# A second Strassen level for three of seven block products, with norm statistics on ScalarE

## The chip, the cores and the metric

The kernel runs on one core of a Trainium2 chip, in float32. The metric is the device time of one execution in microseconds (us). TensorE (PE in the profile) multiplies matrices into the banks of PSUM, VectorE (DVE) and ScalarE (ACT) read and write both PSUM and the on-chip memory SBUF, [...] and SyncE (SP) issues the transfers. Each engine runs its own queue of instructions in order and waits for the others by semaphores.

## The reference, cut to what matters

Sixteen batches of 1024 nodes with 512 features pass two layers that share one 1024x1024 adjacency matrix.

```python
h = relu(layernorm(x))                       # layer 0
x = x + einsum('nm,bmd->bnd', adj, h) @ W0 + bias
h = relu(layernorm(x))                       # layer 1
g = h @ W
e = leaky_relu(g @ a1 [:, None] + g @ a2 [None, :], 0.2) * adj
x = x + elu(softmax(e) @ g + beta * g)
```

The change touches layer 0 and the norm that opens layer 1. There u stands for `relu(layernorm(x))` of layer 0's output.

## The kernel before, in words

Both products of a layer, the one with the adjacency (or the attention matrix) and the one with the weight, are computed by a Strassen scheme of the Winograd form: the left and right factor are cut into 2x2 blocks, seven block products (`PRODUCTS`, p1 to p7) take the place of eight, and sums of blocks (S1, S2, S3, S4 of the left factor, T1 to T4 of the right) are made on VectorE. For layer 0 the first product is `products_a`: h is the left factor (its blocks A11, A12, A22, S1 to S4 are 128x4 chunks of 256 features), the transposed adjacency is the right one (`adjT`), and it stays in SBUF for all sixteen batches. A block product there is two output halves p of four matmuls k, each of 512 columns. The products accumulate in PSUM banks named by kind, Y, W and X, one for each p: p1, p6, p7 and p4 add to Y, p2 to W, p5 and p3 to X. After each half, a reading instruction takes the partial sum out: a ScalarE copy for p1 (into C11), p6 (C12), p5 (C22) and p4 (C21), a VectorE addition for p2, p7 and p3. The second product is `products_b`: its steps, numbered 0 to 13 (product n, half q: 2n+q), are four matmuls of 256 columns each, and VectorE adds every result to the residual tile xr. xr holds x with the bias added.

The order is written by hand. `tc.keep_in_program_order` keeps each engine's instructions as the program has them, and a plan, a table from step numbers to functions, says what other work is issued after which step of a product (-1 is before the first). Batch b's layer 0 is `layer0_a` with the plans of the last batch's output (`plan_out`) and of the next batch's norm (`plan_norm_a`), then `layer0_b` with the rest of that norm (`plan_norm_b`). All of it passes through one helper, line 109, so the profile has line 109 for every instruction and groups are told apart by tile names: y is the first product of layer 0, po its second; z and pq are layer 1's.

The output of layer 0 is handled by `LayerOut`: `keep` stores xr to DRAM as x1, `stats` takes the norm's mean and variance with VectorE's bn_stats and bn_aggr (lines 220 to 223), `inv_std` (212) makes the scale r and the shift nb from them on GpSimd, `relu` writes u to a tile of its own on ScalarE, `logits` multiplies each u chunk with two vectors on VectorE with an accumulator, `sums` makes the left blocks of u, and `store` sends u and its sums to DRAM for layer 1, which runs after all of layer 0. In `plan_out` all four halves of this stand at the start of the next batch.

Of the kernel before, what the change touches and what calls it, by code (L numbers as in the profile page):

```python
# [59 lines left out]
def kernel(  # L60
# [55 lines left out]
        dve.tensor_tensor(o, i0, i1, op=op)  # L116


    def products_a(name, a_blk, b_blk, after):


        c = new_c(name)
        s = {}
        banks = {}
        for n, (prod, an, bn, kind, first, last) in enumerate(PRODUCTS):
            for p in range(2):
                if first:
                    banks[kind, p] = bank(f"{name}_{kind}{p}")
                ps = banks[kind, p]
                for k in range(HC):  # L130
                    pe.matmul(
                        ps, a_blk(an, k)[:, ts(p, P)], b_blk(bn, k),
                        start=(first and k == 0), stop=(last and k == HC - 1),
                        skip_group_check=True,
                    )
                c11, c12, c21, c22 = (c[k][:, p, :] for k in ("C11", "C12", "C21", "C22"))
                if prod == "p1":
                    act.copy(c11, ps)
                elif prod == "p2":
                    add(c11, ps, c11)  # L140
                elif prod == "p6":
                    act.copy(c12, ps)
                elif prod == "p5":
                    act.copy(c22, ps)
                elif prod == "p7":
                    add(c22, ps, c22)
                elif prod == "p3":
                    if not s:
                        for k in ("S1", "S2", "S4"):
                            s[k] = b4.tile([P, 2, 512], F32, tag="b4", name=f"{name}_{k}")  # L150
                    s1, s2 = s["S1"][:, p, :], s["S2"][:, p, :]
                    add(c12, ps, c12)
                    add(s1, c12, c22)
                    add(s2, s1, c11, ALU.subtract)
                    add(c12, c11, c12, ALU.subtract)
                else:
                    act.copy(c21, ps)
                    add(s["S4"][:, p, :], c21, s["S2"][:, p, :], ALU.subtract)
                after(2 * n + p)
        return {  # L160
            "A11": c["C11"], "A12": c["C21"], "S3": c["C12"], "A22": c["C22"],
            "S1": s["S1"], "S2": s["S2"], "S4": s["S4"],
        }

    def new_c(name):
        return {
# [42 lines left out]
        add(t4, b21, t2, ALU.subtract)  # L209


    def inv_std(r, nb, mv):

        k = r.shape[1]
        pool.tensor_scalar(r, mv[:, :, 1], EPS, 1.0, op0=ALU.add, op1=ALU.mult)
        pool.tensor_tensor(r, r, half[:, 0:k], op=ALU.pow)
        pool.tensor_scalar(nb, mv[:, :, 0], -1.0, 1.0, op0=ALU.mult, op1=ALU.mult)
        pool.tensor_tensor(nb, nb, r, op=ALU.mult)
# [6 lines left out]
    class Norm:  # L225


        def __init__(self, name, src, dst):
            self.name, self.src, self.dst = name, src, dst
            self.n = src.shape[1]  # L230

        def stats(self):
            mv = stat.tile([P, self.n, 2], F32, tag="mv", name=f"mv_{self.name}")
            for k in range(self.n):
                stats(mv[:, k, :], self.src[:, k, :])
            self.r = stat.tile([P, self.n], F32, tag="r", name=f"r_{self.name}", bufs=3)
            self.nb = stat.tile([P, self.n], F32, tag="nb", name=f"nb_{self.name}", bufs=3)
            inv_std(self.r, self.nb, mv)

        def relu(self, c=slice(None)):  # L240
            for k in range(self.n):
                act.activation(
                    self.dst[:, k, c], self.src[:, k, c], AF.Relu,
                    scale=self.r[:, k : k + 1], bias=self.nb[:, k : k + 1],
                )

    def node_rows(t, b):

# [12 lines left out]
    def h_stats(b, k):  # L261
# [2 lines left out]
            hs[b, k // 2] = b8.tile([P, HC, D], F32, tag="b8", name=f"h_{b}_{k // 2}")  # L264
        dst = hs[b, k // 2][:, ts(k % 2, 2), :]
        h_norms[b, k] = Norm(f"h{b}_{k}", xs.pop((b, k)), dst)
        h_norms[b, k].stats()

    def h_relu(b, k):
        h_norms.pop((b, k)).relu()  # L270
# [72 lines left out]
    class LayerOut:  # L343
# [16 lines left out]
            sp.dma_start(out=x1d[self.b][nh, q], in_=xr.rearrange("p k d -> p (k d)"))  # L360

        def stats(self, nh, q):
            xr = xrs.pop((self.b, nh, q))
            if not self.us:
                self.s = {
                    n: up.tile([P, HC, HD], F32, tag="up", name=f"u{n}_{self.b}")
                    for n in ("S1", "S2", "S4")
                }
            self.us[nh, q] = up.tile([P, 2, D], F32, tag="up", name=f"u_{self.b}_{nh}_{q}")
            self.norms[nh, q] = Norm(f"u{self.b}_{nh}_{q}", xr, self.us[nh, q])  # L370
            self.norms[nh, q].stats()

        def relu(self, nh, q):
            self.norms[nh, q].relu()

        def logits(self, nh, q):
            junk = self.s["S1"].rearrange("p k d -> p (k d)")[:, 0:D]
            for k in range(2):
                self.logit_parts(4 * nh + 2 * q + k, self.us[nh, q][:, k, :], junk, v_bcs)

# [392 lines left out]
    def logit_weights(k):  # L773

        v = stat.tile([P, DC], F32, tag="v", name=f"v_{k}")
        junk = up.tile([P, D], F32, tag="up", name=f"junk_{k}")
        for dc in range(DC):
            dve.tensor_tensor_reduce(
                out=junk, in0=w1_t[:, dc, :], in1=v_bcs[k], scale=1.0, scalar=0.0,
                op0=ALU.mult, op1=ALU.add, accum_out=v[:, dc : dc + 1],  # L780
            )
        vd[k] = dram.tile([D], F32, name=f"vd_{k}")
# [31 lines left out]
    def plan_first():  # L814
        return {
            1: [(h_sums, 0, 0), (transpose_adj, 0, 1), (transpose_adj, 1, 0), (h_sums, 0, 1)]
            + [(transpose_adj, 1, 1), (adj_sum, "T1"), (adj_sum, "T2")],
            4: [(adj_sum, "T3")], 5: [(adj_sum, "T4")], 7: [(w_sums, w0_c)],
            12: [(add_bias, 0, 0, 0)], 13: [(add_bias, 0, 0, 1)],
        }  # L820

    def plan_out(o, b):

        plan = {
            -1: [(o.keep, 0, 0), (o.stats, 0, 0), (o.keep, 0, 1), (o.stats, 0, 1)],
            0: [(o.relu, 0, 0), (o.keep, 1, 0), (o.stats, 1, 0)],
            1: [(o.relu, 0, 1), (o.keep, 1, 1), (o.stats, 1, 1)],
            2: [(o.relu, 1, 0)], 3: [(o.relu, 1, 1)],
        }

        for i, (nh, q) in enumerate(halves):
            plan.setdefault((4 if b == 1 else 2) + i, []).append((o.logits, nh, q))
        for q in range(2):
            plan.setdefault((8 if b == 1 else 6) + q, []).extend([(o.sums, q), (o.store, q)])
        for i, (nh, q) in enumerate(halves):
            plan.setdefault(3 + i, []).append((load_res, b, nh, q))
            plan.setdefault(6 + i, []).append((add_bias, b, nh, q))
        return plan

    def plan_norm_a(b):  # L840
        return {
            8: [(h_stats, b, 0), (h_stats, b, 1)],
            9: [(h_relu, b, 0), (h_relu, b, 1), (load_x, b, 2), (load_x, b, 3)],
            12: [(h_stats, b, 2)], 13: [(h_stats, b, 3), (h_relu, b, 2)],
        }

    def plan_norm_b(b):
        plan = {0: [(h_relu, b, 3)], 2: [(h_sums, b, 0)], 5: [(h_sums, b, 1)]}
        if b + 1 < B:
            plan[7] = [(load_x, b + 1, 0), (load_x, b + 1, 1)]  # L850
        return plan

    def plan_softmax(order, s):
# [30 lines left out]
        11: {4: "e6", 8: "M6 K6 e7", 11: "M7 K7 x"}, 13: {9: "N n"},  # L884
    }
    FIRST_A = {
        -1: "R0 R1 R2 R3", 2: "B E0", 3: "E1 R4", 4: "E2 R5", 5: "E3 R6 S", 6: "b E4 R7",
        7: "E5", 8: "E6", 9: "E7 s", 10: "D", 12: "T1a", 13: "T1b",
    }
    FIRST_B = {0: "d", 1: "T2a", 2: "T2b", 4: "T3a", 5: "T3b"}  # L890
    LOADS_U = {5: ("U00",), 7: ("U01",), 9: ("U10", "U11"), 11: ("S2",), 13: ("S1", "S4")}


    sms = [Softmax(b) for b in range(B)]
    for b in range(B):
        plans = [plan_first() if b == 0 else plan_out(LayerOut(b - 1), b)]
        if b + 1 < B:
            plans.append(plan_norm_a(b + 1))
            if b == 1:
                plans.append({2: [(logit_weights_back, 0), (logit_weights_back, 1)]})  # L900
            plan_b = merged(plan_norm_b(b + 1), plan_softmax(EARLY_B.get(b, {}), sms[0]))
            if b == 0:
                plan_b = merged(
                    {2: [(add_bias, 0, 1, 0), (add_bias, 0, 1, 1)]}, plan_b,
                    {9: [(logit_weights, 0)], 11: [(logit_weights, 1)]},
                )
        else:
            plans.insert(0, plan_softmax(FIRST_A, sms[0]))
            plans.append({
                8: [(load_u, 0, ("U00", "U01"))],  # L910
                10: [(load_u, 0, ("U10", "U11", "S2", "S1", "S4"))],
            })
            plan_b = merged(plan_softmax(FIRST_B, sms[0]), plan_softmax(LOGITS_B, sms[1]))
        if 0 < b <= G:
            plans.append({13: [(store_mask, b - 1)]})
        layer0_a(b, merged(*plans))
        layer0_b(b, plan_b)


# [67 lines left out]
```

## Time and profile before

| | us |
|---|---|
| median of 3 runs | 2359.93 (2355.52 to 2363.56) |
| profiled execution | 2366.53 |
| its span | 2364.8 |
| TensorE busy | 2336.3 |
| VectorE busy | 1860.9 |
| ScalarE busy | 1072.2 |
| layer 0, one batch in the middle | 72.24 |

The span runs from the first to the last instruction of one profiled execution. Layer 0 takes about the first half of it, 16 batches until 1186 us; layer 1 follows. One matmul of the program is two records in the profile. "Idle before" is the time in which an engine had nothing to do before an instruction, and the arrow names what ended it.

### The profile page before, as it was taken

To read this page: it belongs to the slowest core of one execution; us is meant where nothing else is said; L and a number is where in the kernel's file an instruction comes from. 1 tells how busy PE (TensorE), PEld (TensorE's weight loads), DVE (VectorE), ACT (ScalarE), POOL (GpSimd) and SP (SyncE) were. 2 spreads that over 40 slices of the span, in tenths; PEclk is the share of its full clock that TensorE was granted. 3 is DMA by queue.
4 is the path that set the end of the run, shared out by engine and by line. 5 is a ranking of instruction groups with operands and counts; after the bars stand their busy time and mean duration, and the time that the engine had idled before them with its cause. 6 is when DMAs were issued, how large, how long until landed. Compare 5 with 4: busy or idle time off the path is not lost.

```text
span 2364.8 us, 26003 instructions
## 1 busy us (share of the span) xinstructions
PE 2336.3 (99%) x7264; PEld 1374.3 (58%) x7264; DVE 1860.9 (79%) x3950; ACT 1072.2 (45%) x2675; POOL 561.9 (24%) x732
## 2 busy tenths in 40 slices
PE   9989999999999999999999999999999999999998
PEld 5655566655566655666555666556665566655565
DVE  5788777888888888788968787877877788777774
ACT  3212222222222232222456676667766676666743
POOL 1223323223222233232102221122211222102220
PEclk9999999999999999999999999999999999999999
DMA  6444434434345455345554556555565554565541
GB/s 218 105 150 155 154 117 166 154 125 158 135 145 200 153 174 179 102 148 179 199 189 147 168 190 203 183 166 174 186 211 171 190 159 159 176 191 154 177 125 42
DMA packets 207234, 382.99 MB, mean 162 GB/s; under 512 B 80240, under 2 KB 88432, under 8 KB 207088
## 3 DMA queue, kind: packets, MB, share of 16 engines
q1 hardware_dynamic: 206768, 380.81, 49.8%
q8 instruction: 57, 0.93, 0.2%
q14 instruction: 89, 0.73, 0.1%
q10 hardware_dynamic: 320, 0.52, 0.1%
HBM read 251.92 MB, written 133.50 MB: 163 GB/s over the span
## 4 chain that ended last, share of the span: by engine, by line
PE 63%; DMA 11%; DVE 10%; ACT 10%; SPq 3%; issue 2%; POOL 1%; DVEq 0%; ACTq 0%
PE y_Y L109 18%; PE po_Y L109 9%; PE y_X L109 9%; PE z_Y L109 7%; ACT e L109 5%; PE po_X L109 5%; PE y_W L109 4%; DVE e L109 4%; DMA md<-mx 4%; PE z_X L109 3%; SPq L109 3%; PE pq_Y L109 3%; PE po_W L109 2%; DMA sd<-sm 2%; PE z_W L109 2%
## 5 line engine op out<-in xcount | busy, mean ns | idle before, releaser
L109 POOL TENSOR_TENSOR x<-x,r 128x512 f32<-128x512 f32 x120 | 226.3, 1896 | 899.7 <-DMA ul_S<-ud_S 400.9
L109 ACT ACTIVATE e<-e,nm 128x256 f32<-128x256 f32 x480 | 238.0, 504 | 166.8 <-DVE nm L109 166.8
L109 ACT COPY y_C<-y_Y 128x512 f32<-128x512 f32 x96 | 56.3, 586 | 543.5 <-PE y_Y L109 534.9
L109 DVE CUSTOM_DVE_ANT_0 e<-e,mask 128x256 f32<-128x256 f32 x512 | 233.7, 508 | 77.4 <-DMA mask<-maskd 40.0
L109 DVE CUSTOM_DVE_ANT_0 uS<-u,v_bc 128x512 f32<-128x512 f32 x240 | 242.7, 1011 | 22.7 <-DMA v_bc<-vd 6.3
L109 PE MATMUL y_Y<-adjT_B,h 128*128 128x512 f32 x512 | 226.8, 596 | 2.4 <-ACT adjT_B L109 2.4
L109 PE MATMUL z_Y<-pT,ul_U 128*128 128x512 f32 x512 | 224.9, 592 | 0.0
L109 ACT ACTIVATE e<-s2b,s1b 128x256 f32<-128x256 f32 x512 | 215.3, 512 | 16.1 <-DVE xr L109 16.1
L109 DVE STREAM_TRANSPOSE pT<-e 128x512 f32<-128x512 f32 x240 | 155.8, 688 | 69.3 <-ACT e L109 69.2
L109 ACT ACTIVATE h<-x,nb_h,r_h 128x512 f32<-128x512 f32 (+1 forms) x132 | 98.6, 795 | 225.4 <-POOL nb_h L109 215.1
L109 PE MATMUL pq_Y<-w_c,z_C 128*128 128x256 f32 x768 | 176.8, 381 | 1.3
L109 PE MATMUL po_Y<-w_c,y_C 128*128 128x256 f32 x768 | 173.6, 379 | 0.0
L109 POOL TENSOR_TENSOR xr<-xr,bias_bc 128x1024 f32<-128x1024 f32 x60 | 151.9, 2540 | 68.7 <-DMA xr<-in_x_dram 67.4
L109 PEld LDWEIGHTS y_Y<-adjT_B,h 128*128 128x128 f32 x512 | 97.8, 191 | 119.3 <-issue 115.4
L109 PEld LDWEIGHTS z_Y<-pT,ul_U 128*128 128x128 f32 x512 | 97.3, 190 | 115.6 <-issue 112.4
L109 PEld LDWEIGHTS pq_Y<-w_c,z_C 128*128 128x128 f32 x768 | 144.6, 190 | 32.6 <-issue 7.7
L109 PEld LDWEIGHTS po_Y<-w_c,y_C 128*128 128x128 f32 x768 | 145.9, 190 | 26.7 <-issue 7.7
L109 ACT ACTIVATE r<-z,rs 128x256 f32<-128x256 f32 x192 | 96.1, 500 | 109.6 <-DVE z L109 109.6
L109 DVE TENSOR_TENSOR xr<-po_Y,xr 128x512 f32<-128x512 f32 x128 | 86.4, 688 | 55.5 <-PE po_Y L109 55.5
L109 PE MATMUL po_X<-w_c,y_S 128*128 128x256 f32 x512 | 115.7, 379 | 0.0
L109 PE MATMUL pq_X<-w_c,z_S 128*128 128x256 f32 x512 | 115.6, 379 | 0.0
L109 PE MATMUL y_Y<-adjT_T,h 128*128 128x512 f32 x256 | 112.7, 592 | 1.5 <-DVE y_C L109 1.5
(127 smaller groups left out, 4172.8 us busy)
## 6 DMA issues: line engine op xcount, KB each, us to landing
mask<-maskd SPq DMA_DIRECT2D x128, 512.0 KB
x<-in_x_dram SPq DMA_DIRECT2D x64, 512.0 KB
xr<-in_x_dram SPq DMA_DIRECT2D x256, 128.0 KB
x1d<-xr SPq DMA_DIRECT2D x64, 512.0 KB
ul_U<-ud_U SPq DMA_DIRECT2D x64, 512.0 KB
x<-x1d SPq DMA_DIRECT2D x64, 512.0 KB
out_dram<-x SPq DMA_DIRECT2D x252, 128.0 KB
ud_U<-u SPq DMA_DIRECT2D x60, 512.0 KB
```

The costliest lines, as they stand in the source:

```text
L109: return lambda *args, **kwargs: tc.keep_in_program_order(f(*args, **kwargs))
```

## The change

In batches 1 to 15 of layer 0, p1, p5 and p3 are each computed by the same scheme once more: seven inner products, r1 to r7, each of two matmuls with 256 columns. Their left factors are quarters of the left block and three sums of them (`inner_left`, VectorE, for every batch), their right factors quarters of the adjacency block and three more tiles, which are made once (`inner_right`, `exts`). The result lands in the same banks Y and X, with help of one more bank, y, and for p3 a further one, x. r1, r6 and r7 accumulate in y, and between them ScalarE copies y (after r1), VectorE adds y and an inner sum (after r6), and ScalarE copies y again (after r7); then VectorE adds to the bank of half 0 (after r7) and half 1 (after r3). A paired product, p2, p6 or p7, which stays as it was, gives one matmul between any two inner steps: the matmuls of a group stand in the order r1, plain, r4, plain, r5, plain, r6, plain, plain, r7, plain, r2, plain, r3, plain, and p4 follows the three groups.

The norms' statistics (except those of batch 0 and a late part of the last batch) go from VectorE to ScalarE: sums by an Identity with accumulator, then the squares around the mean by Square. The statistics of layer 0's output are issued from step 11 of the second product on, as the halves become ready, and the last at -1. u is written over xr, so the residual's next load into that buffer comes after u's store. The plans are set anew, and the first softmax's diagonal and sums go from the last batch's first product to its second.

```diff
+    def products_a2(name, a_blk, b_blk, inner, after):
+        read = ReadA(name)
...
+            y = bank(f"{name}_{prod}y")[:, 0:256]
+            x = i0[:, 256:512] if first else bank(f"{name}_{prod}x")[:, 0:256]
+            t = b4.tile([P, 4, 256], F32, tag="b4", name=f"{name}_{prod}t")
...
+            outs = {
+                "r1": (y, True), "r4": (i0[:, 0:256], first), "r5": (x, not first),
+                "r6": (y, False), "r7": (y, False), "r2": (i1[:, 0:256], first),
+                "r3": (i1[:, 256:512], False),
+            }
...
+                if r == "r1":
+                    act.copy(t[:, 0, :], y)
+                elif r == "r5":
+                    act.copy(t5, x)
+                elif r == "r6":
+                    add(t[:, 1, :], y, t5)
+                elif r == "r7":
+                    act.copy(t[:, 2, :], y)
+                    if first:
+                        i0v = i0.rearrange("p (a n) -> p a n", a=2)
+                        add(i0v, i0v, t[:, 2:3, :].to_broadcast([P, 2, 256]))
+                    else:
+                        add(t[:, 3, :], y, t5)
+                        add(i0, i0, t[:, 2:4, :].rearrange("p a n -> p (a n)"))
+                elif r == "r3":
+                    add(i1, i1, t[:, 0:2, :].rearrange("p a n -> p (a n)"))
...
+        for two, one in (("p1", "p2"), ("p5", "p6"), ("p3", "p7")):
+            inn, pla = inner_steps(two), plain_steps(one)
+            for m in range(4):
+                inn[m]()
+                if m == 2:
+                    after(k)
+                pla[m]()
+            pla[4]()
+            if one != "p2":
+                reads(one, 0)
+            inn[4]()
+            pla[5]()
+            reads(two, 0)
+            if one == "p2":
+                reads(one, 0)
+            after(k + 1)
+            inn[5]()
+            pla[6]()
+            after(k + 2)
+            inn[6]()
+            pla[7]()
...
+            after(k + 3)
+            k += 4
...
+    def inner_left(b, prod):
+        left = hs[b][{"p1": "A11", "p5": "S1", "p3": "S4"}[prod]]
+        s = b4.tile([P, 4, 2, P], F32, tag="b4", name=f"in_{b}_{prod}")
...
+        add(s[:, 0], a21, a22)
+        add(s[:, 1], s[:, 0], a11, ALU.subtract)
+        add(a21, a11, a21, ALU.subtract)
+        add(s[:, 2], a12, s[:, 1], ALU.subtract)
...
+        def sums(self):
+            mv = stat.tile([P, 3, self.n], F32, tag="mv", name=f"mv_{self.name}")
+            for k in range(self.n):
+                act.activation(
+                    junk, self.src[:, k, :], AF.Identity, accum_out=mv[:, 0, k : k + 1]
+                )
+            act.activation(mv[:, 1, :], mv[:, 0, :], AF.Copy, scale=-1.0 / D)
+            for k in range(self.n):
+                act.activation(
+                    junk, self.src[:, k, :], AF.Square, bias=mv[:, 1, k : k + 1],
+                    accum_out=mv[:, 2, k : k + 1],
+                )
...
-            self.us[nh, q] = up.tile([P, 2, D], F32, tag="up", name=f"u_{self.b}_{nh}_{q}")
-            self.norms[nh, q] = Norm(f"u{self.b}_{nh}_{q}", xr, self.us[nh, q])
-            self.norms[nh, q].stats()
+            self.us[nh, q] = xr
+            self.norms[nh, q] = Norm(f"u{self.b}_{nh}_{q}", xr, xr)
+            self.norms[nh, q].sums()
...
+        late = 2 if b == 1 else 0
+        plan = {}
+        for k, step in (
+            (-1, (o.stats, 1, 1)), (-1, (o.keep, 0, 0)), (-1, (o.keep, 1, 0)),
+            (-1, (o.keep, 0, 1)), (-1, (o.keep, 1, 1)),
+            (0, (o.relu, 0, 0)), (1, (o.relu, 1, 0)), (2, (o.relu, 0, 1)), (3, (o.relu, 1, 1)),
+            (2 + late, (o.logits, 0, 0)), (3 + late, (o.logits, 1, 0)),
+            (4 + late, (o.sums, 0)), (4 + late, (o.store, 0)),
+            (5 + late, (o.logits, 0, 1)), (5 + late, (load_res, b, 0, 0)),
+            (6 + late, (o.logits, 1, 1)), (6 + late, (load_res, b, 1, 0)),
+            (7 + late, (o.sums, 1)), (7 + late, (o.store, 1)),
+            (8 + late, (load_res, b, 0, 1)), (9 + late, (load_res, b, 1, 1)),
+        ):
+            plan.setdefault(k, []).append(step)
+        for k, (nh, q) in ((9, (0, 0)), (11, (0, 1)), (12, (1, 0)), (13, (1, 1))):
+            plan.setdefault(k, []).append((add_bias, b, nh, q))
...
     def plan_norm_a(b):
-            8: [(h_stats, b, 0), (h_stats, b, 1)],
-            9: [(h_relu, b, 0), (h_relu, b, 1), (load_x, b, 2), (load_x, b, 3)],
-            12: [(h_stats, b, 2)], 13: [(h_stats, b, 3), (h_relu, b, 2)],
+            7: [(h_stats, b, 0)], 8: [(h_stats, b, 1)],
+            9: [(h_relu, b, 0)], 10: [(h_relu, b, 1), (load_x, b, 2)], 11: [(load_x, b, 3)],
...
     def plan_norm_b(b):
-        plan = {0: [(h_relu, b, 3)], 2: [(h_sums, b, 0)], 5: [(h_sums, b, 1)]}
+            0: [(h_stats, b, 2)], 1: [(h_stats, b, 3)], 3: [(h_relu, b, 2)], 4: [(h_relu, b, 3)],
+            5: [(h_sums, b, 0)], 7: [(h_sums, b, 1)], 9: [(inner_left, b, "p1")],
...
+            plan_b = merged(plan_b, {
+                11: [(out_of.stats, 0, 0)], 12: [(out_of.stats, 0, 1)],
+                13: [(out_of.stats, 1, 0)],
+            })
...
+            plans.append({1: [(inner_left, b, "p5")], 5: [(inner_left, b, "p3")]})
+        (layer0_a2 if b else layer0_a)(b, merged(*plans))
```

`ReadA` holds the reading instructions of `products_a`, which are unchanged. `inner_right` is `inner_left` on the adjacency blocks B11, T1 and B22 with 512-wide sums.

## The prediction

> **What bounds the kernel now.** I read the page's totals, then the windows of one batch of layer 0, then the order of time on each engine inside it, then the rows that price an instruction.
>
> ```profile
> PE 2336.3 (99%) x7264; PEld 1374.3 (58%) x7264; DVE 1860.9 (79%) x3950; ACT 1072.2 (45%) x2675; POOL 561.9 (24%) x732
> PE 63%; DMA 11%; DVE 10%; ACT 10%; SPq 3%; issue 2%; POOL 1%; DVEq 0%; ACTq 0%
> ```
>
> TensorE is never idle for long: a matmul saved is time saved, and a wait put on TensorE is time lost. The windows (busy time per engine) cut layer 0 at its period of 72.24 us a batch:
>
> ```profile
> 247.24:319.48 72.24, 72.24 (x225) 42.56 (x225) 58.94 (x110) 16.53 (x24) 20.99 (x37) 1.00 0.47 154
> 608.43:680.67 72.24, 72.24 (x225) 42.56 (x225) 61.79 (x126) 19.74 (x32) 21.26 (x37) 1.00 0.44 145
> ```
>
> TensorE 72.24 of 72.24, VectorE 59, ScalarE 16.5. Two pieces of the chain price the matmuls; one program matmul is two records, so sixteen records are one block product (512 columns) or two steps of the second product (256):
>
> ```profile
> 326.34 6.87 PE y_W L109 x16
> 74.23 3.45 PE po_Y L109 x16
> ```
>
> That is 0.859 us for a 128x512 matmul and 0.43 for a 128x256 one. ScalarE at a batch start (order of time), where it has little to do:
>
> ```profile
> 611.90 0.59 ACT L109 COPY y_C<-y_Y 128x512 f32<-128x512 f32 x1 [21.38 <-PE y_Y L109]
> 612.55 1.52 ACT L109 ACTIVATE u<-xr,nb_u,r_u 128x512 f32<-128x512 f32 x2
> 615.33 0.59 ACT L109 COPY y_C<-y_Y 128x512 f32<-128x512 f32 x1 [1.26 <-PE y_Y L109]
> 615.82 4.34 ACT L109 ACTIVATE u<-xr,nb_u,r_u 128x512 f32<-128x512 f32 x6
> ```
>
> Prices: a group row for an activation with two per-partition operands, then accumulating exponentials in order of time on ScalarE, then logits on VectorE:
>
> ```profile
> L109 ACT ACTIVATE h<-x,nb_h,r_h 128x512 f32<-128x512 f32 x124 | 94.3, 808 | 222.9 <-POOL nb_h L109 212.6 <-DMA ud_U<-u 10.2
> ...
> 1508.19 0.51 ACT L109 ACTIVATE e<-e,nm 128x256 f32<-128x256 f32 x1
> 1508.59 0.20 ACT L109 ACTIVATION_READ_ACCUMULATOR e<-e,nm 128x1 f32 x1
> 1508.69 0.51 ACT L109 ACTIVATE e<-e,nm 128x256 f32<-128x256 f32 x1
> ...
> 780.33 0.69 DVE L109 CUSTOM_DVE_ANT_0 uS<-u,v_bc 128x512 f32<-128x512 f32 x1
> 780.95 0.08 DVE L109 DVE_READ_ACCUMULATOR2_ANT s<- 128x1 f32 x1
> 781.17 0.69 DVE L109 CUSTOM_DVE_ANT_0 uS<-u,v_bc 128x512 f32<-128x512 f32 x1
> ```
>
> An accumulator read starts 0.1 before its activation ends and ends 0.1 after. And TensorE once, after the only long gap in layer 0:
>
> ```profile
> 144.61 3.62 PE L109 MATMUL po_W<-w_c,y_C 128*128 128x256 f32 x16
> 155.15 6.03 PE L109 MATMUL po_Y<-w_c,y_S 128*128 128x256 f32 x16 [6.92 <-DVE xr L109]
> 161.01 3.62 PE L109 MATMUL po_X<-w_c,y_S 128*128 128x256 f32 x16
> ```
>
> A gap of 6.92 us costs another 2.4: the next sixteen take 6.03 for 3.62.
>
> [...]
>
> **The change, part by part.** Only batches 1 to 15 change in steady state.
>
> Removed on TensorE: a product of 8 matmuls of 512 columns (6.87) becomes 7 steps r1 to r7 of two 256-column ones (7 x 0.86 = 6.0). Three products a batch: 2.6 us, in 15 batches 39 us.
>
> VectorE: out go 16 statistics pairs (0.67 + 0.18 each, 13.6). In come twelve 256-wide sums of the inner left factors (three times 1.6 with their waits) and four 256- and six 512-wide additions of the steps (5.8). Net about -3: no loss in sum.
>
> ScalarE: out none; in, per norm half (h and u, 8 a batch), two Identity and two Square with accumulator and one 2-element Copy. [...] I take 3.4. In sum 16.5 + 27 + 4 (nine inner copies) is below 70. So sums hide everything; order does not. All queues run in program order, so I lay the new order out from a batch's start (0), in slots of 0.86:
>
> First group (p1 with p2). r6 (slot 6, due at 5.15) accumulates into the bank that r1 wrote, so it waits for ScalarE's copy of r1. In ScalarE's queue four u statistics stand ahead of that copy. The first needs the residual half finished by step 10 of the second product before, 5.17 before the batch start, and VectorE has 1.6 of inner sums ahead of that addition: it starts at -3.7. Four at 3.4 end at 10.0, the copy at 10.4. **Stall 5.2.**
>
> Then VectorE, idle until now, has in order: r6's addition 0.4; wait for r7 and its copy until 14.3; bank addition 0.7; wait for ScalarE's C11 copy 0.6; C11 0.7; inner sums 1.6; four logits at 0.79, 3.2; second bank and C11 with ScalarE's copy between, 2.0; four logits 3.2; left sums 2.5 (638 to 640 in the trace). It reaches p5's r6 addition at 28.9, done 29.3. p5's r7 waits for that. Without a stall TensorE would be there 18 slots (15.5) after r6, at 25.9. **Stall 3.4**, about 1 of it already at p5's r6, as the last u relu (1.5) precedes that copy.
>
> p5's first bank 31.4, logits 3.2, inner sums 1.6, logits 3.2, second bank: 40.1. ScalarE copies it (40.7), then comes h statistics (44.1), then p3's copy of r1 (44.5). r6 of p3, due at 39.7, waits: **stall 4.9**. Behind a waiting r6 stands all of TensorE's queue; behind ScalarE's copy that waits for VectorE stand the u relus that the logits read, and the next copy of r1, which is how one lateness feeds the next. The rest has room: p4's copies, h statistics 2 and 3 (due by step 5, five microseconds later than ready by the same ledger).
>
> Sum 13.5. Cold clock after gaps near 5 us: between 0 and 2.4 for each of two gaps, since the only example had 6.9; I take 1.5 a batch. Net 15.0 - 2.6 = 12.4, times 15: +186.
>
> Once: 12 inner right sums on VectorE at 0.69, 8.3, in batch 0, where VectorE is busy 123 of 175 us; 0 to 8, I take 2. Last batch: exponentials and transposes of the first softmax stand among these steps (four transposes pairs of 1.4 before the third stall, no h statistics): +4; its moved sums and loads of u hide beside 24 us of products, else some 3 to 10. Together +6.
>
> Costed at nothing: fewer small POOL operations (no one waits at the end of POOL's queue); u in the residual's place, whose next load now waits on SP for u's store. By the ledger the store goes at 43 and the first user, step 1 of the second product, comes at 63; some 20 us cover two transfers. Uncovered, a load late by x delays step 1's addition by x.
>
> Sum: 2366.5 (profiled execution) + 192 = 2558; that execution is 6.6 above the median of 2359.9, so 2552 against the median.
>
> **Rivals.**
> - First stall alone: VectorE catches up because it has 20 us idle in a batch. For: its sum is lower than before. Against: the idle time lies before r6, and the logits cannot pass r6's addition in the queue. 5.2 + 2.4 cold - 2.6 = 5.0 a batch, +81: 2441.
> - Cold after both long gaps: 13.5 + 4.8, and the slow r6 to r7 passes 1 more through the chain; net 16.7, +256: 2616.
> - Faster: TensorE's waits at r6 and r7 are met by earlier instructions than I take, so it does not stall. Place: these six points; it decides where all stalls of a batch sum to less than 2.6. For: TensorE had no such idle time before, under the same helpers. Against: r6 writes what the copy must read first. -39 + 2: 2323.
> - Not doing what it says: the built order has the 14 small matmuls for each of three products, so I give it nothing.
>
> **How the numbers follow.** Main case 0.64 (its own range 2480 to 2610: five statistics on the path, so 0.7 less or 0.8 more of each is 3.5 to 4 us a batch and some 55 in all; the cold clock widens it little), first stall alone 0.13, both cold 0.14, faster 0.05, between (within 0.3%, about what a measurement can tell from no change, or just above) 0.04. Faster 0.06, same 0.02, slower 0.92. The range 2425 to 2635 takes in the second and third case.
>
> **What would show it.** Right: a batch period near 85 us; gaps of TensorE of 3 to 6 us on the y banks, put down to ScalarE's copy at r6 of p1 and p3, to VectorE at r7 of p5; [...] clock under 1.00 in layer 0; layer 1 as before. Wrong: a period under 75, four u statistics done by 5 us, or the logits split around the steps.

## The result, and the profile after

The changed kernel takes 2572.8 us (median; 2566.9 to 2573.9), the kernel before 2361.6 beside it: ratio 1.0894, 95% interval 1.0867 to 1.0921. The profiled span went from 2364.8 to 2571.7. The forecast was slower, 2552 in a range of 2425 to 2635.

The page's totals of the changed kernel (POOL is GpSimd):

```profile
PE 2384.5 (93%) x7804; PEld 1507.3 (59%) x7804; DVE 1794.7 (70%) x3812; ACT 1493.0 (58%) x3890; POOL 535.0 (21%) x612
```

TensorE, busy 99% before, is at 93% of a longer span, and although three block products a batch were made an eighth smaller, its busy time has grown by 48 us: part of its work ran at half the clock, and the mean granted clock is 0.960 where the kernel before has 0.996. VectorE has less to do than before, ScalarE 421 us more.

One batch in the middle (busy time of each engine, then TensorE's granted clock, DMA share and GB/s). It takes 86.15 us instead of 72.24; batches 2 to 14 take 84.3 to 88.6, 86.6 on average:

```profile
608.38:694.53 86.15, 76.52 (x262) 51.91 (x260) 53.93 (x100) 44.65 (x106) 18.90 (x29) 0.92 0.34 117
```

In this batch TensorE is idle 9.6 us, and its clock has fallen from 1.00 to 0.92. Its busy time is 76.5 us, where the plain 72.24 less the 2.6 of saved matmuls is 69.7: 6.9 us are matmuls that ran slower. What it waits for, from the view of waits (us in total, times, longest):

```profile
PE y_p1y L109 <- ACT y_p1t L109: 91.1, 15, 7.9
PE y_p3y L109 <- ACT y_p3t L109: 42.2, 15, 5.3
PE y_p5y L109 <- DVE y_p5t L109: 29.6, 14, 3.6
PE y_p5y L109 <- ACT y_p5t L109: 3.5, 14, 0.3
PE y_p3x L109 <- DVE in_p L109: 2.3, 1, 2.3
```

All five are on the scratch banks of the second level: 168.7 us together. From the first matmul of batch 1 to the first of layer 1, the changed kernel takes 1310.1 us (91.29 to 1401.38), the kernel before 1095.1 (91.34 to 1186.47): 215.0 more. Of these, 163.4 is idle time (171.8 us against 8.4 in the kernel before). The other 51.6 is busy time, though 38.7 of matmul time was saved: some 90 us, or 6.0 a batch, is slower matmuls and not waiting.

TensorE in order of time, the same batch; the bracket holds the idle time ahead of a row and who ended it:

```profile
619.18 2.08 PE L109 MATMUL y_p1y<-ext,in_p 128*128 128x256 f32 x4 [5.47 <-ACT y_p1t L109]
621.04 3.27 PE L109 MATMUL y_W<-adjT_B,h 128*128 128x512 f32 x4
624.15 1.03 PE L109 MATMUL y_p1y<-adjT_B,h 128*128 128x256 f32 x4
...
639.75 1.13 PE L109 MATMUL y_p5y<-adjT_T,hS 128*128 128x256 f32 x4 [2.00 <-DVE y_p5t L109]
640.71 1.71 PE L109 MATMUL y_Y<-adjT_T,hS 128*128 128x512 f32 x2
...
653.95 1.51 PE L109 MATMUL y_p3y<-ext,in_p 128*128 128x256 f32 x4 [1.91 <-ACT y_p3t L109]
655.25 3.24 PE L109 MATMUL y_Y<-adjT_B,h 128*128 128x512 f32 x4
658.32 1.03 PE L109 MATMUL y_p3y<-adjT_B,hS 128*128 128x256 f32 x4
```

The three stalls stand where the prediction put them: r6 of p1, r7 of p5, r6 of p3. After each, the same tile operation takes up to twice its time: four records on a y bank 2.08 us for 1.03, four with 512 columns 3.27 for 1.88. This is the part that isn't waiting, and in this batch it follows the short gaps of 2 us as well as the one of 5.5. ScalarE in order of time shows what r6 of p1 waited for:

```profile
605.06 0.63 ACT L109 ACTIVATE junk<-xr 128x512 f32<-128x512 f32 x1 [10.45 <-issue]
...
606.80 0.72 ACT L109 ACTIVATE junk<-xr,mv_u 128x512 f32<-128x512 f32 x1
...
608.50 0.63 ACT L109 ACTIVATE junk<-xr 128x512 f32<-128x512 f32 x1
...
618.77 0.35 ACT L109 COPY y_p1t<-y_p1y 128x256 f32<-128x256 f32 x1
```

Four statistics stand in a row from 605.06; the second begins at 608.50, so one takes 3.44 us. The copy of r1, whose matmuls were done by 609.4, ends at 619.12.

### The profile page after: what moved, and what is told of

It is laid out like the page before. It is cut to its first block, busy times and chain, and to the rows that moved or that the text cites. A ratio compares the mean times of both kernels' runs of the same rounds, so it can differ in the third digit from the quotient of the medians.

```text
span 2571.7 us, 27837 instructions
## 1 busy us (share of the span) xinstructions
PE 2384.5 (93%) x7804; PEld 1507.3 (59%) x7804; DVE 1794.7 (70%) x3812; ACT 1493.0 (58%) x3890; POOL 535.0 (21%) x612
## 5 line engine op out<-in xcount | busy, mean ns | idle before, releaser
L109 DVE CUSTOM_DVE_ANT_0 e<-e,mask 128x256 f32<-128x256 f32 x512 | 234.1, 509 | 70.5 <-DMA mask<-maskd 39.1
L109 DVE CUSTOM_DVE_ANT_0 uS<-xr,v_bc 128x512 f32<-128x512 f32 x240 | 167.6, 698 | 6.3
L109 PE MATMUL y_Y<-adjT_B,h 128*128 128x512 f32 (+1 forms) x332 | 168.2, 615 | 2.4 <-ACT adjT_B L109 2.4
L109 ACT ACTIVATE junk<-xr 128x512 f32<-128x512 f32 x120 | 75.6, 630 | 151.3 <-issue 146.6
L109 PE MATMUL y_W<-adjT_B,h 128*128 128x512 f32 x256 | 146.5, 674 | 0.0
L109 POOL TENSOR_SCALAR r_h<-mv_h 128x2 f32<-128x2 f32 x64 | 13.8, 215 | 594.7 <-ACT junk L109 583.8
L109 PE MATMUL y_Y<-adjT_T,hS 128*128 128x512 f32 x256 | 135.7, 627 | 0.0
L109 DVE TENSOR_TENSOR y_p1t<-y_p1y,in_p 128x256 f32<-128x256 f32 x15 | 6.4, 425 | 180.2 <-PE y_p1y L109 180.2
```

The costliest lines, as they stand in the source:

```text
L109: return lambda *args, **kwargs: tc.keep_in_program_order(f(*args, **kwargs))
```

## The experiments

The kernels are the changed one with the edit shown, except the one that measures gaps, and the versions at the end, which build on one another. Ratios are to the kernel before on the same chip.

### Statistics and moved steps without the second level

```diff
-        (layer0_a2 if b else layer0_a)(b, merged(*plans))
+        layer0_a(b, merged(*plans))
```

and no steps inner_right and inner_left.

> Second level taken out (seven plain block products in every batch, no inner sums); statistics stay on ScalarE, u stays in the residual's place, the moved steps stay where the change has them. Theory (the stalls come from inner steps that need a copy or an addition a few microseconds after it is issued): no gaps on TensorE's banks, a period of 72.2 us as before, median within 15 us of 2362. Rival (statistics on ScalarE, u in place or the moved steps cost by themselves): a period above 74, median over 2395.

Measured: 2358.2 us, ratio 0.9998 (0.9991 to 1.0005). The steady batch is 72.24 us as before, and TensorE's longest wait in the whole run is this one:

```profile
PE po_Y L109 <- DVE xr L109: 2.4, 1, 2.4
```

So the statistics on ScalarE (busy 1451.6 us in this run for 1072.2 before), u in the residual's place and the new order of steps cost nothing in a steady batch beside plain products. At the two ends they change something, and it cancels in part: batch 1 takes 72.2 us where the kernel before, with its wait of 6.9 there, takes 83.5, and the last batch takes 78.8 for 72.5. The loss of the changed kernel needs the second level, whose steps turn a copy or an addition around within a few microseconds.

### The first stall alone: two u statistics back on VectorE

```diff
-            self.norms[nh, q].sums()
+            self.norms[nh, q].stats() if nh else self.norms[nh, q].sums()
```

> Two of the four u statistics, those of the second node half, back on VectorE; the other two and all h statistics stay on ScalarE. Theory (queue order on ScalarE makes the first stall): r6 of p1 no longer waits, which takes away 5.5 of gap and about 2.4 of cold clock a batch; r7 of p5 has VectorE's addition about in time by the same ledger, since VectorE also starts about 7 earlier; the wait of p3's r6 for the copy behind the h statistics stays (2 to 2.5, and 1.8 of cold clock). Period 75 to 78, median 2400 to 2455. Rival 1 (the first stall only moves to VectorE): period over 82, median over 2510. Rival 2 (all three stalls are one chain that the first one feeds): period under 71.5, median under 2350.

Measured: 2477.4 us, ratio 1.0494 (1.0458 to 1.0529): 95 us less than the changed kernel, and 22 above the interval that the theory gave (the profiled execution took 2466.1). TensorE's waits in this run:

```profile
PE y_p3y L109 <- ACT y_p3t L109: 48.1, 15, 6.6
PE y_p5y L109 <- DVE y_p5t L109: 29.6, 14, 3.6
```

The 91.1 us of the first stall are gone, so the queue of ScalarE made it. What missed is the second stall, expected to go as well: it has the same 29.6 us in the same 14 waits. In order of time on TensorE:

```profile
584.32 1.03 PE L109 MATMUL y_p1y<-adjT_B,h 128*128 128x256 f32 x4
...
599.91 1.13 PE L109 MATMUL y_p5y<-adjT_T,hS 128*128 128x256 f32 x4 [2.00 <-DVE y_p5t L109]
...
614.10 1.52 PE L109 MATMUL y_p3y<-ext,in_p 128*128 128x256 f32 x4 [1.90 <-ACT y_p3t L109]
```

From r7 of p1 to r7 of p5 is 15.59 us here and 15.60 in the changed kernel; to r6 of p3 it is 29.78 and 29.80. So neither later stall is fed by the first. VectorE cannot begin its work for p1's banks before r7 of p1, and from there its list and ScalarE's are of fixed length, whatever came earlier.

### The second stall alone: the left sums later

```diff
-            (4 + late, (o.sums, 0)), (4 + late, (o.store, 0)),
+            (5 + late, (o.sums, 0)), (5 + late, (o.store, 0)),
```

> Only the left sums of u's first half, and their stores, moved from before r6's addition of p5 to after p5's r7. Theory (the second stall is the four left sums, 2.5 us, that stand ahead of r6's addition in VectorE's queue): the wait of p5's r7 for VectorE (29.6 us over 14 waits) goes nearly to nothing, the first stall stays at 6 a batch; 2 of gap and 1.8 of cold clock less, period about 82.5, median about 2515. Rival (VectorE is as late one step on, so the wait returns at p3): the waits at p3 grow by as much, median 2555 to 2575.

Measured: 2579.5 us, ratio 1.0932 (1.0916 to 1.0949): no gain; it is 7 us slower, though the two intervals just overlap. The rival holds in what it says of the waits, though the time is 4.5 above its interval too. The first stall's 91.1 us are unchanged; the wait at p3:

```profile
PE y_p3y L109 <- ACT y_p3t L109: 87.5, 15, 7.0
```

The second stall is gone and the third has grown by 45.3, more than the second one held. From r7 of p1 to r6 of p3 it is 30.05 us (623.78 to 653.83), against 29.80: VectorE's list up to that point is as long as before, and the 2.0 us of waiting and the slow matmuls after it, 1.7 us in the changed kernel, have only turned into waiting further on.

### The third stall alone: h statistics one step later

```diff
-            7: [(h_stats, b, 0)], 8: [(h_stats, b, 1)],
-            9: [(h_relu, b, 0)], 10: [(h_relu, b, 1), (load_x, b, 2)], 11: [(load_x, b, 3)],
+            8: [(h_stats, b, 0)], 9: [(h_stats, b, 1)],
+            10: [(h_relu, b, 0), (load_x, b, 2)], 11: [(h_relu, b, 1), (load_x, b, 3)],
```

> The changed kernel with only the h statistics 0 and 1 of the next batch (and their applications) one step later, behind ScalarE's copies of r1 and r5 of p3. Theory (the third stall is one h statistics of 3.4 us that stands ahead of p3's copy of r1 in ScalarE's queue): the wait of p3's r6 for ScalarE (42.2 us over 15) goes, 2.1 of gap and 1.8 of cold clock less a batch, period about 82, median about 2515. Rival (that copy is late because VectorE's addition into p5's second bank is late): the wait stays above 30 us, median 2555 to 2575.

Measured: 2521.8 us, ratio 1.0688 (1.0670 to 1.0706), 51 us less than the changed kernel. The waits at p1 (91.1) and p5 (29.6) are unchanged; at p3:

```profile
PE y_p3y L109 <- ACT y_p3t L109: 9.1, 9, 6.6
```

The third wait falls from 42.2 to 9.1, most of that in the last batch (6.6). From r7 of p1 to r6 of p3 is now 26.95 us (603.55 to 630.50). So the one h statistics ahead of the copy made this stall: without it the distance is 2.85 shorter, and a wait of 0.3 is left in a steady batch.

### All statistics back on VectorE

```diff
-            self.norms[nh, q].sums()
+            self.norms[nh, q].stats()
-        if b:
-            h_norms[b, k].sums()
-        else:
-            h_norms[b, k].stats()
+        h_norms[b, k].stats()
```

> All statistics of u and h back on VectorE, at the places in the order where the change has them; second level and u in place stay. Theory (queue order): no wait of r6 for ScalarE; one new wait of p3's r7 for VectorE, about 3 and 1.8 of cold clock, since two h statistics (1.7 each) and the left sums stand ahead of r6's addition; period about 74.5, median near 2400. Rival (VectorE, with 54 + 13.6 of some 70 us, becomes the bound and is late everywhere): period 78 or more, waits for VectorE at every y bank, median 2450 to 2520.

Measured: 2462.1 us, ratio 1.0427 (1.0409 to 1.0444), in the rival's interval, as is the period of 78.41 (591.46 to 669.87). Its largest waits:

```profile
PE y_p3y L109 <- DVE y_p3t L109: 35.0, 14, 5.5
PE y_p5y L109 <- DVE y_p5t L109: 29.6, 14, 3.6
PE y_p1y L109 <- DVE y_p1t L109: 12.0, 5, 5.6
```

But VectorE is busy only 65.8 of those 78.4 us: it is late at three points, not at its limit. The second stall is again 29.6, though a different set of instructions came before p1's r7. So having ScalarE take the statistics is not the whole of the loss: with them on VectorE the second level loses 4.3% in place of 8.9%, at other places. The theory, which expected one new wait and some 2400 us, fails.

### What a gap costs in clock

A burst of 24 matmuls (256 columns), then 64, after gaps set by a chain of VectorE additions:

```diff
+    for size in (23, 63):
+        for turn in range(4):
+            for n in (0, 16, 1, 12, 2, 9, 3, 7, 4, 6, 5):
+                gap(n)      # n + 2 dependent additions
+                burst(size) # one matmul that needs the chain, then size others
```

> A kernel of another kind: it computes nothing of the reference. Bursts of 24 (then of 64) 128x256 float32 matmuls, 10.3 us (27.5 us) each when warm, separated by gaps that a chain of 2 to 18 dependent VectorE additions sets (about 1.0 to 7.9 us), four times each. Read is the loss: the time of the burst that follows a gap, less its warm time. Theory A (the one of the prediction: only long gaps cost)[...]. Theory B (as the trace of the changed kernel reads): 1 to 2 us lost already after a gap of 2 us, 2.4 after 5 us and no more after 8. Theory C (the losses after short gaps in the changed kernel have another cause): no loss after any gap below 5 us.

Three gaps, in order of time on TensorE:

```profile
142.00 0.70 PE L83 MATMUL head<-xt,w 128*128 128x256 f32 x2 [1.76 <-DVE w L83]
142.53 10.09 PE L83 MATMUL main<-xt 128*128 128x256 f32 x46
...
172.93 1.22 PE L83 MATMUL head<-xt,w 128*128 128x256 f32 x2 [2.22 <-DVE w L83]
173.94 11.26 PE L83 MATMUL main<-xt 128*128 128x256 f32 x46
...
204.26 1.22 PE L83 MATMUL head<-xt,w 128*128 128x256 f32 x2 [2.68 <-DVE w L83]
205.28 12.65 PE L83 MATMUL main<-xt 128*128 128x256 f32 x46
```

After 1.76 us the burst takes 10.62 from its first start to its last end, after 2.22 it takes 12.27, after 2.68 it takes 13.67. All eleven gaps, as loss against the undisturbed burst (four repeats of each agree within 0.04, but for three first repeats after long bursts, which lost 0.5 to 1.1 more and are left out of the table):

| gap, us | 0.8 | 1.3 | 1.8 | 2.2 | 2.7 | 3.1 | 3.6 | 4.1 | 5.0 | 6.4 | 8.2 |
|---|---|---|---|---|---|---|---|---|---|---|---|
| loss after 10.6 us bursts | 0 | 0 | 0 | 1.65 | 3.0 | 1.4 | 2.9 | 1.7 | 2.5 | 2.2 | 2.6 |
| loss after 27.9 us bursts | 0 | 0 | 0 | 0 | 0 | 2.85 | 2.6 | 2.4 | 1.7 | 1.4 | 1.45 |

Theory A, the one that the prediction used, does not hold: gaps of 2.2 us cost 1.65 in the first row. That only long gaps cost was the author's estimate. Theory B does not hold as a rule of the gap's length either, since 2.2 and 2.7 cost nothing in the second row, and 8.2 us between long bursts lost 2.5 the first time and 1.45 afterwards. What decides is in the clock's own record. In all traces of this case the granted clock is either 1.00 or 0.50, and it changes only at the steps of a grid of 3.41 us that does not follow the program: stretches at 0.50 last one, two or three such slices. Here are slices of that grid, with TensorE's busy time, its records, its clock, DMA share and GB/s, two of this run around the gap of 2.22, and two around one of 2.68 between long bursts:

```profile
169.49:172.90 3.41, 1.22 (x6) 1.00 0.00 0
172.90:176.31 3.41, 3.38 (x8) 0.50 0.00 0
...
1033.06:1036.47 3.41, 1.44 (x7) 1.00 0.00 0
1036.47:1039.89 3.42, 2.71 (x13) 1.00 0.00 0
```

The gap of 2.22 lay nearly whole in one slice, which was idle for 2.19 us, and the next slice had half the clock. The gap of 2.68 was split: 1.97 us in one slice, 0.71 in the next, and the clock stayed at 1.00. In the changed kernel the clock falls in the same way, at the first stall and at p5's r7:

```profile
613.60:617.01 3.41, 0.10 (x1) 1.00 0.00 0
617.01:620.43 3.42, 1.25 (x3) 0.50 0.00 0
620.43:623.84 3.41, 3.41 (x6) 0.50 0.00 0
...
637.49:640.91 3.42, 1.42 (x6) 1.00 0.38 152
640.91:644.32 3.41, 3.41 (x7) 0.50 0.89 288
```

Counted over all slices of all traces, the start of each kernel aside, a slice at full clock with more than 2.0 us of idle time was followed by one at half the clock, and one with less than 1.9 was not (between the two both occur, as the ends of matmuls are modelled). The loss of a burst is about half of the time that it ran at 0.50: 3.38 us at 0.50 after the gap of 2.22, and 1.65 lost. So the ups and downs of the table, and the difference between its rows, come from where each gap fell on the grid; the repeats agree because a turn of eleven gaps comes to last a whole number of slices (51 with the short bursts, 174.1 us). A gap of 2 us can cost nearly as much again, or nothing. In the changed kernel the gap of 2.0 us at p5's r7 costs 1.7 in nine steady batches and nothing in four. In the run with the h statistics moved, it is the same gap, and the row behind it runs at full speed:

```profile
619.59 1.13 PE L109 MATMUL y_p5y<-adjT_T,hS 128*128 128x256 f32 x4 [2.00 <-DVE y_p5t L109]
620.55 1.02 PE L109 MATMUL y_Y<-adjT_T,hS 128*128 128x512 f32 x2
```

### A version aimed below both

Two u statistics on VectorE, h statistics one step later, and, in batches 2 to 15, VectorE's list between r7 of p1 and r6 of p3 cut apart, with a new place for steps between r6 and r7:

```diff
+            after(k + 0.5)
             inn[4]()
...
+    (0, (o.relu, 0, 0)), (0, (o.relu, 1, 0)), (0.5, (o.logits, 0, 0)),
+    (1, (o.relu, 0, 1)), (2, (o.relu, 1, 1)), (3, (o.logits, 1, 0)),
+    (4.5, (o.sums, 0)), (4.5, (o.store, 0)),
...
+    (6, (o.logits, 0, 1)),
...
+    (7, (o.logits, 1, 1)), (8.5, (o.sums, 1)), (8.5, (o.store, 1)),
```

> A version aimed below both kernels: two u statistics on VectorE, h statistics one step later, and in batches 2 to 15 the logits and left sums laid around the inner steps (logits between r6 and r7 of p1, one pair after p1, left sums between r6 and r7 of p5 and of p3, the other two pairs of logits in p5's last step and after it), so that no copy of r1 and no addition of r6 has another step of over 1.5 us ahead of it when it is due. Theory (all of the loss is queue order, and without it the second level gives 2.6 us a batch): period 69.7 to 71, with batch 1 and the last batch still stalled, median 2330 to 2352. Rival (with VectorE and ScalarE this full the lateness only moves to other steps): period 73 to 77, median 2370 to 2430.

Measured: 2413.5 us, ratio 1.0231 (1.0215 to 1.0247), with a steady batch of 74.8. The three stalls are gone in the steady batches; the rival is right that one more turned up behind them. TensorE's largest wait, then VectorE in order of time ahead of what it waited for, and GpSimd at that time:

```profile
PE y_Y L109 <- DVE y_C L109: 39.9, 14, 3.1
```

```profile
589.08 0.68 DVE L109 TENSOR_TENSOR uS<-xr,uS 128x512 f32<-128x512 f32 x1
589.90 2.31 DVE L109 COPY s2t<-s 128x8 f32<-128x8 f32 x1
...
594.26 2.16 DVE L109 TENSOR_TENSOR y_S<-y_C,y_C 128x512 f32<-128x512 f32 x1
...
598.27 0.68 DVE L109 TENSOR_TENSOR y_C<-y_Y,y_C 128x512 f32<-128x512 f32 x1
```

```profile
589.84 2.35 POOL L109 TENSOR_TENSOR xr<-xr,bias_bc 128x1024 f32<-128x1024 f32 x1
593.51 2.36 POOL L109 TENSOR_TENSOR xr<-xr,bias_bc 128x1024 f32<-128x1024 f32 x1
```

p4's second half adds into the bank that the row at 598.27 must read first. That row stands behind the left sums (2.5 us) and two rows of 0.2 and 0.7 us that took 2.3 and 2.2 while GpSimd added biases.

The next version moved the left sums ahead of p3's r6, the logits' store to the end of the product and two bias additions behind the h statistics, and kept batch 1 and the last batch plain:

```diff
-    (7, (o.logits, 1, 1)), (8.5, (o.sums, 1)), (8.5, (o.store, 1)),
-    (9, (add_bias, b, 0, 0)), (11, (add_bias, b, 1, 0)),
+    (7, (o.logits, 1, 1)), (7, (o.sums, 1)), (7, (o.store, 1)),
+    (10, (add_bias, b, 0, 0)), (10, (add_bias, b, 1, 0)), (13, (o.store_logits,)),
...
-        (layer0_a2 if b else layer0_a)(b, merged(*plans))
+        (layer0_a2 if 1 < b < B - 1 else layer0_a)(b, merged(*plans))
```

> The version before it, with its one remaining wait taken out: p4's second half waited 3.05 us for VectorE's read of p7's second half, which stood behind the left sums (2.5 us) and a small copy that took 2.3. Now the second half's left sums stand after the logits, ahead of p3's r6, where VectorE had 1.6 idle; the logits' store goes to the end of the adjacency product and two bias additions of GpSimd behind the h statistics. The second level is used in batches 2 to 14 alone, as batch 1 and the last one stalled. Theory (all of the loss is queue order): period of those batches 69.7 to 70.6, the other batches as before, median 2328 to 2342. Rival (the lateness moves on once more): period over 72.2, median over 2360.

Measured: 2347.3 us, ratio 0.9947 (0.9930 to 0.9964), 5 above the theory's interval, with the expected 70.5 in seven of its thirteen batches with the second level. It can't stand as a result: its plain batches 1 and 15 multiply with right factors that the second level has changed, so part of its output is not the reference's. The last step is to prepare the right factors where they are needed and take them back before the last batch:

```diff
+    def inner_back(prod):
+        r = adjT[{"p1": "B11", "p5": "T1", "p3": "B22"}[prod]]
+        b12, b22 = r[:, 0:2, 256:512], r[:, 2:4, 256:512]
+        add(b12, b22, b12, ALU.subtract)
```

> The version before it with the right factors put right: they are prepared in batch 1, whose own products are plain, and in batch 14 three additions give the plain ones back for the last batch (the version before left the last and the second batch with changed factors, so part of its output is not the reference's; the work and its order are otherwise the same). Theory (all of the loss is queue order, the second level is worth its 2.6 us a batch less about 1 of waits that are left): period 70.5 in batches 2 to 14, no cold clock, median 2340 to 2352. Rival (the prepared factors on VectorE in batch 1 and the three additions in batch 14 delay TensorE): median over 2356.

Measured: 2349.7 us, ratio 0.9959 (0.9944 to 0.9973): below both kernels, by 0.4% against the one before and by some 8.7% against the changed one (2349.7 to 2572.8). One of its batches, and the three places of the old stalls in order of time:

```profile
311.31:381.81 70.50, 70.12 (x262) 49.23 (x261) 59.69 (x108) 38.77 (x88) 21.62 (x31) 1.00 0.47 157
```

```profile
316.47 1.03 PE L109 MATMUL y_p1y<-ext,in_p 128*128 128x256 f32 x4
...
331.96 1.03 PE L109 MATMUL y_p5y<-adjT_T,hS 128*128 128x256 f32 x4
...
342.29 1.03 PE L109 MATMUL y_p3y<-ext,in_p 128*128 128x256 f32 x4
...
364.44 3.72 PE L109 MATMUL po_Y<-w_c,y_S 128*128 128x256 f32 x16 [0.38 <-DVE xr L109]
```

No bracket at the first three, clock 1.00, and a period of 70.50: 1.74 under the kernel before. Not all of the calculated 2.6 arrives: of the 0.84 that are missing, 0.65 lies at the wait of 0.38 and the rows next to it (sixteen records of the second product, 3.45 from start to start elsewhere, take 4.00 and 3.55 there). Thirteen such batches would gain 23 us and gain 13, because six of them take 71.2 to 73.7 us, some with a wait of 0.87 at r7 of p1. The two plain batches at the ends nearly cancel: batch 1 is 6.2 shorter than in the kernel before, as its wait of 6.9 has become 3.1, and the last batch, with a wait of 4.0, is 8.4 longer. In all, 10 us arrived.

## Why the prediction was right, point by point

The forecast names the cause that the experiments show: stalls of TensorE on the y banks, made by what stands ahead of a copy or an addition in another engine's queue. Its number is close partly by luck, since it put the stalls too high and the slow clock too low by similar amounts.

**What bounds the kernel: right.** TensorE, busy 99% before, has no slack, so waits put on it count in full. That plain products leave the other engines ample slack is shown by the ratio of 0.9998 with ScalarE busy 379 us longer.

**Matmul saving of 2.6: right in kind.** The reordered version, the last one of the experiments, has 1.74 of it.

**Statistics at 3.4 each: right.** 3.44 measured; the group means are 630 ns (Identity) and 721 ns (Square). The 3.4 was the author's estimate, and so was the 0.4 of a 256-wide addition or copy in the forecast's ledger: the means in the changed kernel are 0.42 and 0.36.

**Stall 1, 5.2: right.** 91.1 us over 15, or 6.1; 5.5 in seven of the steady batches, 6.2 to 7.9 in the other six. In the batch shown the copy was forecast to be done 10.4 us after the start; it was at 10.74 (619.12 less 608.38).

**Stall 2, 3.4, and stall 3, 4.9: right in place, too large.** They measured 2.25 (0.25 and 2.00) and 1.9 to 2.5, or 3.6 where stall 2 cost no clock. The ledger of VectorE and ScalarE was close: the addition that r7 of p5 waits for was put at 29.3 and ended at 31.3, p3's copy of r1 was put at 44.5 and ended at 45.5. What failed more is the other half of each difference, the time at which TensorE would be there: put at 25.9 and 39.7, it came at 29.4 and 43.7. Of the 3.5 at the first, 2.4 is slow matmuls; of the 4.0 at the second, 1.8 is slow matmuls and 2.1 is that r7 of p5 itself came later. Time that the slow clock takes before such a point is not waited there again. The four steady batches in which stall 2 cost no clock show it: there p3's r6 waits 3.6.

**One lateness feeds the next: wrong for these stalls.** With the first one taken out, the distance from p1's r7 to p3's r6 stays at 29.8, and the second stall at 29.6 us.

**Cold clock, 1.5 a batch: wrong.** The prediction gave nothing to the gap of 3.4 and 1.5 together to the two near 5. The slow matmuls measured 6.9 in the batch shown, and 6.0 more than before on average over the fifteen. It had one example, a gap of 6.92, and no case of a short one; the gap of 2.0 us at p5's r7 cost 1.7 in the nine batches in which it lay in one slice of the clock's grid, and nothing in the four in which it was split (at most 1.95 in one).

Cutting the batch at p1's r7 and p3's r6, with the reordered version as the one without these stalls:

| stretch, us | changed | reordered | more |
|---|---|---|---|
| first matmul to r7 of p1 | 15.77 | 7.74 | 8.0: 5.6 late start, 2.4 clock |
| r7 of p1 to r6 of p3 | 29.80 | 23.24 | 6.6: 4.2 waits, 2.4 clock |
| r6 of p3 to the next batch | 40.58 | 39.52 | 1.1: 1.8 clock, less 0.7 lost at a wait in the other |
| period | 86.15 | 70.50 | 15.65 |

The two errors nearly cancel, since in the middle stretch the points at which VectorE and ScalarE finish set the length, however it is shared between waiting and slow matmuls. The forecast had 15.0 over a batch of 69.7 (13.5 of stalls and 1.5 of clock); this batch has 16.5 over it (9.6 and 6.9).

**Once, +6: too low at the end, and a term of batch 1 left out.** Batch 0 ends at 91.29 against 91.34, so its 2 cost nothing. The last batch takes 96.3 us for 72.5 before, 10 beyond what a steady batch loses, where 4 was said; without the second level it is already 6.3 longer than before. Batch 1 was priced like the others, but takes 88.0 for 83.5, only 4.5 more, because the new order removes the wait of 6.92 that the kernel before has there. Layer 1, forecast as before, is 8 us shorter in this execution (1170.3 for 1178.3). In the eight other kernels of this document with its moved steps it takes 1171 to 1177, so most of the 8 is scatter between executions; whether a few microseconds of it belong to the change stays open.

**Costed at nothing: right in a steady batch.** Fewer GpSimd operations, u in the residual's place and the later loads: 72.24 us, and a ratio of 0.9998, with all of them.

**The rivals.** First stall alone (2441) falls with 78 us of other waits, and with the run that takes this stall out and still loses 4.9%. Cold after both long gaps (2616) had the clock nearer right, and named its passing through r6 and r7, but added it on top of stalls that it shortens. Faster (2323) named the right condition: all stalls under 2.6 in sum. The changed order doesn't meet it; the reordered one does.

## What to carry to other kernels

A scheme that saves matmuls by adding copies and additions with a short turn-round needs not free engines but free places in their queues: ask for each such copy what stands ahead of it and when that can begin. Work out the other engines' finishing times from the last point at which they had to wait for TensorE; between two such points a stall can be moved but not removed unless their list gets shorter. A gap of TensorE can cost more than its own length: in these runs it cost another 1.4 to 3.0 us in clock when some 2 us of idle time lay in one slice of 3.41 us, so that the same gap of 2.0 us cost 1.7 in nine batches and nothing in four.

## What was not expected of the hardware

- TensorE's clock was granted in slices of 3.41 us, at 1.00 or 0.50, on a grid that does not follow the program. Half the clock followed a slice with more than 2.0 us of idle time, not one with less than 1.9. So the same gap cost 1.7 us in one batch and nothing in another (2.0 us at p5's r7), and the loss (1.4 to 3.0 us between the bursts) did not grow with the gap. That the place on the grid decides is read from the clock's record in the kept traces; no run was made that shifts a gap by itself.
- Some of VectorE's instructions took longer while GpSimd added a bias. In the kernel before, thirteen additions with both operands in SBUF (y_S<-y_S,y_C) took 2.87 to 2.89 us there and 0.69 elsewhere; those with one operand in a PSUM bank (y_C<-y_W,y_C) took 0.68 to 0.69 at such times too. In the first of the versions at the end an addition with both operands in SBUF took 2.16 at such a time. The 128x8 copy with one operand (0.17 us alone) took 2.31 in the batch shown; what delayed it the trace does not tell.
